# First image of an attention kernel: the next image's input load moves from unit 12 to unit 16, and its group-norm steps get new distances

## The chip, the cores and the metric

The kernel runs on one core of one Trainium2 chip. A core has a matrix engine (TensorE, "PE" in the profile, with its weight loads as "PEld"), three engines for elementwise work (VectorE "DVE", ScalarE "ACT", GpSimd "POOL"), and SyncE ("SP"), which issues DMA transfers. The metric is the device time of one execution in microseconds; lower is better. A unit below is a step of the kernel's inner loop, not a piece of hardware.

## The reference, cut to what matters

Eight images of 384 channels by 32x32 pixels pass through two attention layers; the second has a feed-forward part. The change touches the first layer alone:

```python
def _gn(v, G=32, eps=1e-5):
    g = v.reshape(B_, G, C_ // G, H_, W_)
    m = jnp.mean(g, axis=(2, 3, 4), keepdims=True)
    s = jnp.var(g, axis=(2, 3, 4), keepdims=True)
    return ((g - m) / jnp.sqrt(s + eps)).reshape(v.shape)
...
tokens = x.reshape(b, c, n).transpose(0, 2, 1)          # n = 1024 tokens, c = 384
qkv = (tokens @ qkv_w + qkv_b).reshape(b, n, 3, NUM_HEADS, HEAD_DIM)   # 8 heads of 48
attn = jnp.einsum('bhnd,bhmd->bhnm', q * scale, k)
attn = attn + _relative_bias(h, w, mlp_w1, mlp_b1, mlp_w2, mlp_b2)[None]
attn = jax.nn.softmax(attn, axis=-1)
out = jnp.einsum('bhnm,bhmd->bhnd', attn, v)
...
x = x + _L0_conv_ref(_gn(x), ...)
```

`_relative_bias` is a small network over the difference of two pixel positions. It gives one number for each head and each pair of row and column difference, so its whole output follows from a table of 8 x 63 x 63 values.

## The kernel before, in words

The program is one stream for each engine, written out by hand: the order in which the Python code calls operations is the order in which each engine gets them, and each engine works through its own stream in that order. Waits between engines are semaphores.

The first layer is `_layer0`. It handles the images one after the other. For each image it makes 32 units: 4 pairs of heads, times 2 halves of the 1024 queries, times 4 groups of 256 keys. In unit `i`, `scores` (L685 to L711) emits 16 matmuls on PE into two PSUM tiles `s` (L692), then the 16 matmuls of `weigh` for the unit two before (probabilities times v into `o`, L723), then for each of the two heads an add of the position bias on DVE (L703, `e<-s,grow`) and an exponential on ACT (L707). All PSUM tiles of this kind, 4 of them, come from one pool (`mm2`): two `s` tiles per unit and one `o` tile that lives for four units. So PE can only run one unit ahead of the adds on DVE. After the last key group of a query half, ACT copies one half of `o` out (L731) and DVE adds the other (L734).

Work beside the attention is hung into a list, `later`. `later.after(n, work)` calls `work` at the n-th `later.step()` from there, and each unit ends with one such step; what is registered during unit `i` with n = 1 is therefore called at the end of unit `i` itself. What is called at the end of a unit stands on every engine behind that unit's adds and exponentials. For the first image (b = 0) this is:

- The bias table turned into `grow`, the form the adds read. The 32 pieces (8 heads times 4) are loaded from DRAM with four DMAs each (`grow_load`, L486), and then reversed by one copy (`grow_turn`), on ACT for even pieces (L496) and on DVE for odd ones (L498). The last 16 pieces (0 to 15 below) are staged in slices of `oT`, the last four of them in two slices by turns, so that each must wait for the turn of the piece two before it. Piece 13 is loaded at the end of unit 12 and turned at the end of unit 14; piece 14 follows one unit later; piece 15 is loaded at the end of unit 14 and turned at the end of unit 16. Then there is nothing left of the table.
- The qkv weights are cut into three parts for later products (`_cut_weights`): the steps L108, L134, L112 and L142 on DVE, each in a unit of its own from unit 9 on, and stores to DRAM (L122).
- For each pair of heads, `divide` sends the softmax sums through DRAM (L749, L751, L756, L764), with a power (L752) and a multiplication (L768) on POOL.
- The next image: `load` (L343) issues three DMAs of 512 KB into `xn1`. `group_norm` (L501) returns seven steps: three that measure one third each with two statistics instructions on DVE (L513), the third of which also sends the statistics through DRAM to regroup them (L517, L521); `scatter`, which combines them (L527 on DVE, four small POOL instructions from L528) and sends scale and offset back through DRAM (L535, L539); and three that apply them to one third each on ACT (L551). At units 28, 29 and 31 `mask` (L108) reads the normalised image, and after the 32 units it is projected.

All DMAs named here are issued by SP, in one queue and in program order, each on one of eight completion semaphores in turn: a DMA waits until the one eight before it has landed.

Which units the seven steps fall in before: the load at unit 12 with distances 5, 6, 7, 10, 13, 14, 15 puts the measurements at the ends of units 16, 17 and 18, `scatter` at 21, the applications at 24, 25 and 26.

## Time and profile before

| | us |
|---|---|
| median of 3 runs | 2976.45 (2976.02 to 2978.29) |
| the profiled execution | 2973.66 |
| its span, first to last instruction | 2971.8 |
| PE busy in the span | 2940.6 (99%) |
| DVE busy | 1940.2 (65%) |
| ACT busy | 1507.2 (51%) |
| POOL busy | 489.8 (16%) |
| first image's 32 units | from about 75 to 193 in the span |

The median and the profiled execution are two different measurements: the span comes from the profiled one, which was 2.79 us below the median of the timed ones. Engine shares are averages over the whole program. Times with two decimals in the prediction are positions in the span, in us from its start. [...] the start of the first matmul of a unit is the useful mark.

### The profile page before, as it was taken

What the parts mean: (1) busy time and instruction counts of PE and PEld (TensorE: products, weight loads), DVE (VectorE), ACT (ScalarE), POOL (GpSimd) and SP (SyncE); (2) the same over time, 40 slices, a digit from 0 to 9 for tenths busy, and PEclk for the clock granted to TensorE, in tenths of its full rate; (3) what the DMA queues carried; (4) which work ended last, traced back from release to release, by engine and by line L of the source; (5) the groups of instructions that cost most, each with busy time, mean ns of one, the idle gap of its engine ahead of it and who ended that gap; (6) DMA issues with size and microseconds to landing.
All of it is one profiled execution on the core that took longest, in us unless ns stands there. A gap on an engine that the chain in (4) does not pass through costs nothing.

```text
span 2971.8 us, 47061 instructions
## 1 busy us (share of the span) xinstructions
PE 2940.6 (99%) x19370; PEld 1662.5 (56%) x19370; DVE 1940.2 (65%) x1937; ACT 1507.2 (51%) x1846; POOL 489.8 (16%) x312
## 2 busy tenths in 40 slices
PE   8999999999999999999999999999999999999998
PEld 3345555656565655644545656746747747655553
DVE  3775748575675747564565785775775775875756
ACT  2654626354453626354463564564564555564644
POOL 3020202111110202112202202301302302302020
PEclk9999999999999999999999999999999999999999
DMA  7532131312203130222411112202202112112111
GB/s 196 171 99 85 44 111 38 97 59 52 76 16 112 24 104 24 63 89 60 128 50 38 61 38 67 85 17 79 73 25 77 68 31 71 67 40 82 40 45 38
DMA packets 129520, 203.71 MB, mean 69 GB/s; under 512 B 61872, under 2 KB 79648, under 8 KB 128816
## 3 DMA queue, kind: packets, MB, share of 16 engines
q1 hardware_dynamic: 126032, 198.77, 22.9%
q8 instruction: 156, 2.56, 0.4%
q10 hardware_dynamic: 3264, 1.82, 0.2%
q14 instruction: 68, 0.56, 0.1%
HBM read 152.99 MB, written 38.51 MB: 64 GB/s over the span
## 4 chain that ended last, share of the span: by engine, by line
PE 91%; DVE 3%; DMA 2%; ACT 2%; issue 1%; SPq 0%; POOL 0%; DVEq 0%; ACTq 0%
PE s L692 15%; PE o L723 14%; PE s L1649 11%; PE o L1698 10%; PE pg L170 6%; PE y2p L1943 6%; PE y1p L1892 5%; PE pp L791 4%; PE pv L666 4%; PE pv L1586 4%; PE pm L170 3%; PE pp L1795 3%; PE pq L1438 1%; PE pq L572 1%; DMA rb<-rd 1%
## 5 line engine op out<-in xcount | busy, mean ns | idle before, releaser
L707 ACT ACTIVATE e<-e 128x1024 f32<-128x1024 f32 x512 | 535.3, 1057 | 357.0 <-DVE e L703 339.9
L703 DVE TENSOR_TENSOR e<-s,grow 128x1024 f32<-128x1024 f32 x512 | 601.2, 1218 | 164.4 <-PE s L692 156.5
L692 PE MATMUL s<-qk 48*64 48x512 f32 x4096 | 615.0, 592 | 7.6 <-DVE e L703 7.5
L723 PE MATMUL o<-e,v 64*64 64x512 f32 x4096 | 609.1, 590 | 0.0
L1660 ACT ACTIVATE e<-s,kc 128x512 f32<-128x512 f32 x768 | 463.9, 694 | 173.0 <-PE s L1649 163.4
L1649 PE MATMUL s<-qk,qk 64*64 64x512 f32 x3072 | 418.9, 592 | 1.8 <-DVE oT L1708 1.6
L1698 PE MATMUL o<-e,v 64*64 64x512 f32 x3072 | 414.5, 590 | 0.0
L692 PEld LDWEIGHTS s<-qk 48*64 48x64 f32 x4096 | 228.9, 132 | 250.9 <-issue 104.3
L723 PEld LDWEIGHTS o<-e,v 64*64 64x64 f32 x4096 | 244.8, 133 | 196.9 <-issue 113.8
L1649 PEld LDWEIGHTS s<-qk,qk 64*64 64x64 f32 x3072 | 154.0, 132 | 191.9 <-issue 109.2
L1675 DVE TENSOR_TENSOR t<-t,e 128x1024 f32<-128x1024 f32 x192 | 230.9, 1221 | 45.8 <-ACT e L1660 45.8
L1698 PEld LDWEIGHTS o<-e,v 64*64 64x64 f32 x3072 | 159.9, 133 | 168.9 <-issue 141.8
L752 POOL TENSOR_TENSOR inv<-sums,over 128x16 f32<-128x16 f32 x32 | 95.6, 2988 | 866.3 <-DMA sums<-sd 591.4
L1879 DVE TENSOR_REDUCE parts<-y 128x1 f32<-128x1024 f32 x75 | 89.7, 1217 | 103.4 <-ACT y L1876 103.0
L1672 DVE TENSOR_TENSOR t<-e,e 128x1024 f32<-128x1024 f32 x96 | 114.1, 1224 | 59.5 <-ACT e L1660 59.5
L1555 POOL TENSOR_TENSOR hc<-hc,rsqrt 128x32 f32<-128x32 f32 x24 | 138.2, 5757 | 2.0
L666 PE MATMUL pv<-wv,xn 128*128 128x384 f32 x384 | 128.9, 490 | 0.0
L1586 PE MATMUL pv<-wv,bx 128*128 128x384 f32 x384 | 128.3, 491 | 0.0
L1795 PE MATMUL pp<-oT,L_attn_proj_wT 128*128 128x512 f32 x288 | 126.3, 595 | 1.5 <-DVE oT L1761 1.5
L791 PE MATMUL pp<-oT,wp 128*128 128x512 f32 x288 | 125.7, 595 | 0.0
L650 DVE SCALAR_TENSOR_TENSOR qk<-pg,qk 128x1024 f32<-128x1024 f32 x42 | 51.5, 1225 | 112.8 <-PE pg L170 98.1
L1586 PEld LDWEIGHTS pv<-wv,bx 128*128 128x128 f32 x384 | 119.4, 314 | 9.8 <-ACT e L1660 4.1
(213 smaller groups left out, 3507.7 us busy)
## 6 DMA issues: line engine op xcount, KB each, us to landing
rb<-rd SPq DMA_DIRECT2D x110, 256.0 KB
wc<-there SPq DMA_DIRECT2D x25, 576.0 KB
wc<-cut SPq DMA_DIRECT2D x24, 576.0 KB
xn<-in_x_dram SPq DMA_DIRECT2D x24, 512.0 KB
res<-in_x_dram SPq DMA_DIRECT2D x24, 512.0 KB
x<-res SPq DMA_DIRECT2D x24, 512.0 KB
bx<-x SPq DMA_DIRECT2D x8, 1536.0 KB
rq<-hi SPq DMA_DIRECT2D x48, 256.0 KB
```

What stands on the lines that cost most here:

```text
L170: self.nc.tensor.matmul(out[:, h], w[:, i, k], part[k][:, ts(h, HALF)], start=(k == 0 and i != 1), stop=(k == KC - 1 and i != 0),)
L666: nc.tensor.matmul(pv[:, i, 0:C], xn[:, k, ts(2 * m2 + i, P)], wv[:, k, :], start=(k == 0), stop=(k == KC - 1),)
L692: nc.tensor.matmul(s[j][ts(c, QP), i], qk[pair][rows, 1, ts(4 * m2 + 2 * i + c, QP)], qk[pair][rows, 0, ts(h, HALF)], start=True, stop=True,)
L703: nc.vector.tensor_add(e.rearrange("p (i q) -> p i q", i=2), s[j], bass.AP(near.tensor, near.offset, [near.ap[0], [-QROWS * IW, 2], [1, HA ...
L707: nc.scalar.activation(e, e, AF.Exp)
L723: nc.tensor.matmul(po[ts(j, S0), r], v[keys, 2 * m2 + i, 2 * pair + j, :], es[j][keys, ts(i, HALF)], start=(m2 == 0 and i == 0), stop=(m2 ...
L791: nc.tensor.matmul(pps[b, m][:, h], (wp[:, k] if k < NF0 else wl)[:, ts(m, P)], oT[:, k, ts(h, HALF)], start=(k == 0), stop=(k == (NF0 if ...
L1586: nc.tensor.matmul(pv[:, i, 0:C], xt[:, k].rearrange("c (p m) -> c m p", m=MT)[:, 2 * m2 + i], wv[:, k], start=(k == 0), stop=(k == KC - 1),)
L1649: nc.tensor.matmul(s[j][ts(c, QP), i], qk[pair, 1][rows, ts(4 * m2 + 2 * i + c, QP)], qk[pair, 0][rows, ts(h, HALF)], start=True, stop=True,)
L1660: nc.scalar.activation(e[:, ts(i, HALF)], s[j][:, i], AF.Exp, scale=kc[:, pair, j, m : m + 1])
L1675: nc.vector.tensor_add(total[j], total[j], e)
L1698: nc.tensor.matmul(po[ts(j, D1), r], v[keys, 2 * m2 + i, at : at + D1], es[j][keys, ts(i, HALF)], start=(m2 == 0 and i == 0), stop=(m2 == ...
```

## The change

In the loop over the units of the first layer, for the first image alone, the load of the next image is issued at unit 16, not 12, and the seven steps of its group norm get shorter distances. Images from the second on keep their unit and their distances.

```diff
-                if i == (12 if b == 0 else 1) and b + 1 < B:
+                if i == (16 if b == 0 else 1) and b + 1 < B:
                     xn = load(b + 1)
                     for at, stage in zip(
-                        (5, 6, 7, 10, 13, *((14, 15) if b == 0 else (13, 13))),
+                        (3, 4, 5, 7, 9, 10, 11) if b == 0 else (5, 6, 7, 10, 13, 13, 13),
                         group_norm(b + 1, xn),
                     ):
                         later.after(at, stage)
```

The measurements come to the ends of units 18, 19 and 20 (16, 17 and 18 before), `scatter` to 22 (21 before), and the applications stay at the ends of 24, 25 and 26.

## The prediction

> **What bounds the kernel now.** The page first: PE carries the program.

> ```profile
> PE 2940.6 (99%) x19370; PEld 1662.5 (56%) x19370; DVE 1940.2 (65%) x1937; ACT 1507.2 (51%) x1846; POOL 489.8 (16%) x312
> PE 91%; DVE 3%; DMA 2%; ACT 2%; issue 1%; SPq 0%; POOL 0%; DVEq 0%; ACTq 0%
> L692 PE MATMUL s<-qk 48*64 48x512 f32 x4096 | 615.0, 592 | 7.6 <-DVE e L703 7.5
> ```

> So only PE's idle or slowed time can be won. Of its 7.5 us of waits before L692, the longest is 4.2. The waits between 105 and 200 us place it:

> ```profile
> DVE grow L498 <- DMA oT<-table: 4.9, 1, 4.9
> PE s L692 <- DVE e L703: 4.7, 2, 4.2
> SPq L486 <- DMA xn<-in_x_dram: 3.5, 3, 1.9
> ```

> DVE waited 4.9 us for one piece of the bias table, and PE then waited 4.2 us for DVE. The chain of waits has the same place on the path, and the timelines of DVE, PE and SP show what stood there:

> ```profile
> 125.28 6.37 DMA oT<-table
> ...
> 131.73 0.65 DVE L498 COPY grow<-oT 128x480 f32<-128x480 f32 x1 [4.92 <-DMA oT<-table]
> ...
> 128.38 0.59 PE L692 MATMUL s<-qk 48*64 48x512 f32 x1
> ...
> 133.57 2.83 PE L692 MATMUL s<-qk 48*64 48x512 f32 x11 [4.17 <-DVE e L703]
> ...
> 138.76 0.76 PE L692 MATMUL s<-qk 48*64 48x512 f32 x1
> ...
> 119.53 1.98 SPq L764 DMA_DIRECT2D rb<-rd  x2
> 121.94 1.31 SPq L343 DMA_DIRECT2D xn<-in_x_dram  x3
> 123.36 7.23 SPq L486 DMA_DIRECT2D oT<-table  x8
> ```

> Piece 13 (the first four of those eight L486 DMAs) was issued at 123.36 to 125.28, behind the three xn DMAs, and its last DMA landed 6.37 us later. Its turn at the end of unit 14 holds DVE, behind it wait the adds of unit 15, and behind them, for a PSUM tile, the scores of unit 16. The windows of one microsecond give the second half of the cost:

> ```profile
> 131.00:132.00 1.00, 0.00 (x0) 0.00 (x0) 0.27 (x1) 0.00 (x0) 0.00 (x0) 1.00 0.66 187
> 132.00:133.00 1.00, 0.00 (x0) 0.00 (x0) 1.00 (x2) 0.00 (x0) 0.00 (x0) 0.64 0.97 289
> 133.00:134.00 1.00, 0.43 (x4) 0.30 (x8) 1.00 (x2) 0.39 (x1) 0.00 (x0) 0.50 0.67 213
> 138.00:139.00 1.00, 1.00 (x12) 0.39 (x8) 1.00 (x2) 0.39 (x1) 0.00 (x0) 0.50 0.00 0
> 139.00:140.00 1.00, 1.00 (x12) 0.29 (x8) 1.00 (x2) 0.93 (x2) 0.00 (x0) 0.94 0.06 16
> ```

> (Columns: stretch, its length, busy time of PE, PEld, DVE, ACT and POOL, granted clock, DMA share, GB/s.) The clock fell to half at about 132.3 and came back at about 139.1, so PE worked at half speed for 5.5 us after it started again.

> [...] the DMAs of piece 14 wait on the semaphores of xn, and were issued at 126.67, 128.11 and 130.29, so the three thirds had landed 4.7, 5.7 and 7.4 us after their issues.

> **The change part by part.**

> *The load leaves unit 12.* The first scores matmul of a unit comes every 3.44 us where nothing disturbs (149.79, 153.23, 156.67). From unit 16's to unit 17's it took 138.76 - 128.38 = 10.38. The disturbance cost 6.94 us: the 4.17 of idle PE, plus half of 5.5 (2.75), which is 6.92. Would piece 13 be in time? Its DMAs now follow the rb DMAs at once (else they wait only for turn 11, done at 120.06): 121.6 to 123.3. rb had landed when POOL's multiplication started at 125.28. Bytes: 120 to 125 us moved 232 GB/s, 1.16 MB; what is due in front of and with piece 13 is two rb DMAs (0.52 MB), about 0.2 MB of piece 12 and its own 0.47 MB, so its last byte moves at about 125.1; before, data ended about 2 us ahead of the 131.65 landing; so it lands by about 127.2. The turn also carries a wait on POOL's multiplication into oT, which ended at 127.66. DVE reaches it at 126.8 (adds of unit 14: 124.46 + 2.36). The wait thus falls from 4.92 to 0.4 to 0.9; the turn (0.64) ends by about 128.3, against about 127.95 at which unit 15's adds are due. That is 0.3 late, nearly covered by the slack below. I charge 0.2, from 0 (landed by 126.8) to 1.5 (landed at 128.8). Pieces 14 and 15 have room: their issues wait for turns 12 (125.34) and 13 (128.3), last DMAs at about 127.1 and 130.1, plus 2 to 3 us, against turns at about 131.1 (ACT) and 133.9 (DVE).

> *The load enters unit 16.* On SP it now stands behind the weight store of unit 15 (L142 on DVE ends at about 130.7): issued at about 131.2 to 132.5, 1.3 us of issuing. With the landings seen (4.7, 5.7, 7.4), in company of piece 15, the thirds are there at 136, 137 and 139. DVE wants them after the adds of units 18, 19, 20: about 140.9, 144.4, 148. Nearly 5 us to spare, so 0; cover gone, each us beyond goes to DVE. Queued behind it on SP are the L749 DMAs of pair 1, which wait for DVE at the end of unit 17 anyway; the second rb DMA, a weight store and the statistics DMA now wait for the semaphores of xn, 10 us or more after its issue.

> *Measurements at 18, 19, 20 and scatter at 22.* The same six L513 (0.68 each, 1.2 a pair when chained) and one L527 (0.79, chained 0.71) move among other DVE work. Adds take 2.26 of a unit's 3.44, so 1.18 is free, and extra work pushes PE only past that and past about 0.45 of slack (scores end to first add's end 1.2, against 1.72 of weigh matmuls between). Excess over 1.18, before: unit 16 (turn 0.57 + pair 1.2) 0.59; 17 (L734 0.6 + 0.1 + pair) 0.72; 18, 0.02; sum 1.33, less slack 0.88. Unit 21 (0.1 + 0.6 + L134 0.87 + 0.71) 1.10, less slack 0.65. Together 1.5; measured, units 17 to 24 took 25.64 against 7 x 3.44 = 24.08, 1.56, of which about 0.28 belongs to the two o evictions, so 1.28. After: 18 and 19, 0.02 each; 20 (L108 0.46 + pair) 0.48; 21 (0.7 + 0.87) 0.39; 22 (L112 0.87 + 0.71) 0.40; sum 1.31, less one slack 0.86. Gain 0.4 to 0.7; I take 0.5, bounds 0 and 1.

> *Chains through DRAM.* The statistics' way from last L513 to the combined instruction took 4.9 us in image 0 (8.21 to 13.09, waiting); now the adds of two units, L734, L134 and L112 stand between, 6.9 us: 2.0 to spare. From L527 to the applied third it took 5.8 (13.09 to 18.88, waiting); now 24's exponentials end 10.3 after the adds of 22 start, and L527 starts at 3.1: 7.2, so 1.4 to spare. A late one would hold ACT only, two units ahead of the weigh matmuls. POOL's multiplication of pair 1 (2.4 to 3.7 us) now stands ahead of the four small ones; its rb lands about 2.7 us before it would matter. Cost 0 for all.

> *Sum.* -6.94 - 0.5 + 0.2 = -7.2. Span 2971.8 - 7.2 = 2964.6; its execution 2973.66 - 7.2 = 2966.5. The timed median lies 2.8 above that execution; I subtract from it as it is: 2976.45 - 7.2 = 2969.3.

> **Rivals.**

> *Half of it (gain 3 to 5.9).* [...] if the idle 4.17 us usually don't drop the clock in the timed runs, only 4.17 + 0.5 - 0.2 = 4.5 is there: 2972.0. Or piece 13 lands at 129 behind rb and its turn still holds DVE by over 1 us. [...] Against it: [...] the timed runs are no faster than the profiled one.

> *A new wait takes its place (slower).* If xn's first third needs more than 9.7 us from its issue, unit 18's measurement holds DVE as the turn did, and the clock may fall again. At 9.7 + 0.45 + 7.2 = 17 us it eats the gain; about 13 more on DVE than today's slack, 23 us in all, would make it slower by over 0.2%: 2983. Against it: 7.4 us for all three in a fuller queue, and 3.6 us for the first third at the start of the kernel (0.74 to 4.36).

> *It does nothing (2975 to 2977).* The chain would have to show the stall covered by something else that ends just then: POOL's multiplication ended at 127.66, four microseconds earlier. Little speaks for it.

> **How the numbers follow.** Full gain (6 to 8.5 us) 0.66; half 0.23; nothing 0.05; slower 0.06. A measurement tells about 0.2% from no change, 5.95 us here, so the full gain is just outside and half of it inside: faster 0.67, same 0.27, slower 0.06. The likeliest one's own range is 2968 to 2970.5. For 8 in 10 I take in the half case and a full gain with a longer slow-clock stretch in the timed runs (up to 6.8 us at half speed, 3.4): 2967 to 2974.

> **What would show it.** Right: no wait of L498 on the table over 1 us near 127, no PE wait of 4 us, granted clock 1.00 from 125 to 145, unit 16's to unit 17's scores 3.4 to 3.8 us, L513 without a DMA wait, units 18 to 24 with about 0.9 us over the pace. Wrong: DVE idle before L513, L527 or L498 by microseconds; a slow clock elsewhere; or everything as described and the timed median less than 5 us lower, which would say that the timed runs didn't pay the slow clock.

## The result, and the profile after

The changed kernel takes 2969.5 us in the median of nine runs (2967.66 to 2970.98). The kernel before, run beside it, takes 2976.45 in nine (2974.22 to 2979.95). The ratio is 0.9975, 95% interval 0.9964 to 0.9985, so the change makes the kernel 6.95 us faster; 2969.3 was predicted.

The two profiled executions show less than that: 2973.66 before and 2970.98 after, with spans of 2971.8 and 2969.1. The first lies below all nine runs of the kernel before, the second is the highest of the nine of the changed kernel. The first image is therefore compared stage by stage here; what may make executions scatter by microseconds comes at the end.

The page of the changed kernel, the lines that answer to those shown before:

```profile
PE 2939.3 (99%) x19370; PEld 1667.5 (56%) x19370; DVE 1941.8 (65%) x1937; ACT 1506.5 (51%) x1846; POOL 490.0 (17%) x312
PE 91%; DVE 3%; DMA 2%; issue 2%; ACT 1%; POOL 0%; SPq 0%; DVEq 0%; ACTq 0%; POOLq 0%
L692 PE MATMUL s<-qk 48*64 48x512 f32 x4096 | 612.2, 591 | 5.1 <-DVE e L703 5.0
```

PE still carries the program. The idle time in front of L692 fell from 7.6 to 5.1 and its busy time from 615.0 to 612.2: less waiting, and fewer matmuls at half clock (6.83 us of it in the first layer before, none now). It fell by less than the 4.2 of the stall because this execution has a wait of 1.5 us in a later image. The waits between 105 and 200 us (total, times, longest) show that the stall is gone:

```profile
DVE grow L498 <- DMA oT<-table: 0.9, 1, 0.9
PE s L692 <- DVE e L703: 0.4, 2, 0.2
```

DVE waits 0.9 us for piece 13, not 4.9; PE's longest wait for DVE is 0.2, not 4.2. The timelines of DVE, PE and SP (start, duration, engine, line) at the same place:

```profile
128.46 0.65 DVE L498 COPY grow<-oT 128x480 f32<-128x480 f32 x1 [0.92 <-DMA oT<-table]
...
141.43 1.28 DVE L513 BATCH_NORM_STATS2 gst<-xn 128x6 f32<-128x512 f32 x2
...
129.11 0.59 PE L692 MATMUL s<-qk 48*64 48x512 f32 x1
...
132.95 0.59 PE L692 MATMUL s<-qk 48*64 48x512 f32 x1
...
122.94 4.85 SPq L486 DMA_DIRECT2D oT<-table  x8
...
132.35 1.75 SPq L343 DMA_DIRECT2D xn<-in_x_dram  x3
```

From unit 16's first scores matmul to unit 17's it is 132.95 - 129.11 = 3.84 us (10.38 before). The image is issued at 132.35, and the measurement L513 at 141.43 starts without a wait. The windows of three microseconds (stretch, length, busy time of PE, PEld, DVE, ACT and POOL, granted clock, DMA share, GB/s):

```profile
128.00:131.00 3.00, 2.84 (x28) 0.82 (x24) 2.54 (x3) 1.36 (x2) 0.86 (x1) 1.00 0.91 247
131.00:134.00 3.00, 3.00 (x32) 1.08 (x28) 2.56 (x4) 2.34 (x4) 0.00 (x0) 1.00 0.77 230
134.00:137.00 3.00, 3.00 (x32) 0.92 (x24) 2.41 (x4) 1.71 (x2) 0.00 (x0) 1.00 1.02 325
```

The clock stays at 1.00 where it was 0.50 from about 132.3 to 139.1, and the DMA engines are no less busy than before (0.90 over these 9 us, 0.79 in the same ones before): the image now moves while nobody waits for it.

By stages of the first image, from first scores matmul to first scores matmul, with two later executions of the changed kernel that are told of below:

| us | before | after | after, again | after, third |
|---|---|---|---|---|
| unit 16 to 17 (the stall) | 10.38 | 3.84 | 3.44 | 3.44 |
| unit 17 to 25 (statistics) | 29.08 | 28.90 | 29.22 | 28.95 |
| gain of both | | 6.72 | 6.80 | 7.07 |

All of the gain is in the first row. The second one, from which the prediction wanted 0.5, gained 0.18, lost 0.14 and gained 0.13. Its ends are the first scores matmuls of units 17 and 25; that of unit 25 before, then after:

```profile
167.84 0.59 PE L692 MATMUL s<-qk 48*64 48x512 f32 x1
```

```profile
161.85 0.59 PE L692 MATMUL s<-qk 48*64 48x512 f32 x1
```

### The profile page after: what moved, and what is told of

It is laid out like the page before. It is cut to its first block, busy times and chain, and to the rows that moved or that the text cites. A ratio compares the mean times of both kernels' runs of the same rounds, so it can differ in the third digit from the quotient of the medians.

```text
span 2969.1 us, 47062 instructions
## 1 busy us (share of the span) xinstructions
PE 2939.3 (99%) x19370; PEld 1667.5 (56%) x19370; DVE 1941.8 (65%) x1937; ACT 1506.5 (51%) x1846; POOL 490.0 (17%) x312
## 4 chain that ended last, share of the span: by engine, by line
PE 91%; DVE 3%; DMA 2%; issue 2%; ACT 1%; POOL 0%; SPq 0%; DVEq 0%; ACTq 0%; POOLq 0%
PE s L692 14%; PE o L723 14%; PE s L1649 11%; PE o L1698 10%; PE pg L170 6%; PE y2p L1943 6%; PE y1p L1892 5%; PE pp L791 4%; PE pv L666 4%; PE pv L1586 4%; PE pm L170 3%; PE pp L1795 3%; PE pq L1438 1%; PE pq L572 1%; DMA rb<-rd 1%
## 5 line engine op out<-in xcount | busy, mean ns | idle before, releaser
L703 DVE TENSOR_TENSOR e<-s,grow 128x1024 f32<-128x1024 f32 x512 | 601.1, 1218 | 161.9 <-PE s L692 152.3
L692 PE MATMUL s<-qk 48*64 48x512 f32 x4096 | 612.2, 591 | 5.1 <-DVE e L703 5.0
L692 PEld LDWEIGHTS s<-qk 48*64 48x64 f32 x4096 | 229.0, 132 | 246.0 <-issue 101.0
L752 POOL TENSOR_TENSOR inv<-sums,over 128x16 f32<-128x16 f32 x32 | 96.0, 2999 | 857.5 <-DMA sums<-sd 584.8
L1586 PE MATMUL pv<-wv,bx 128*128 128x384 f32 x384 | 128.3, 491 | 0.0
```

The costliest lines, as they stand in the source:

```text
L692: nc.tensor.matmul(s[j][ts(c, QP), i], qk[pair][rows, 1, ts(4 * m2 + 2 * i + c, QP)], qk[pair][rows, 0, ts(h, HALF)], start=True, stop=True,)
L703: nc.vector.tensor_add(e.rearrange("p (i q) -> p i q", i=2), s[j], bass.AP(near.tensor, near.offset, [near.ap[0], [-QROWS * IW, 2], [1, HA ...
L1586: nc.tensor.matmul(pv[:, i, 0:C], xt[:, k].rearrange("c (p m) -> c m p", m=MT)[:, 2 * m2 + i], wv[:, k], start=(k == 0), stop=(k == KC - 1),)
```

## Experiments

The main theory: the three image DMAs, issued ahead of piece 13 of the bias table, delay that piece; its turn holds DVE, DVE holds PE, and the pause costs once more through the clock. The rivals: what helped is the new place of the statistics; or only the idle time is paid and not the clock; or the piece is late not because it stands behind the image in the queue but because both share the DMA engines' bandwidth. After a pause, half clock lasted 3.41 us (in the changed kernel, from 2034.84) or 6.83 (in the kernel before, from 132.28); a stretch of 3.41 is called a window of half clock below.

### One half of the edit at a time

The new units of the statistics (18, 19, 20 and 22), with the load left at unit 12:

```diff
-                        (5, 6, 7, 10, 13, *((14, 15) if b == 0 else (13, 13))),
+                        (7, 8, 9, 11, 13, 14, 15) if b == 0 else (5, 6, 7, 10, 13, 13, 13),
```

> The load stays at unit 12, only the group norm's steps take the new units (18, 19, 20, 22; applications as before). Main theory (the gain is the table piece freed from the image in front of it): the turn of piece 13 waits for the table 4.5 to 5.2 us as before, PE is idle about 4 us, the clock drops to half for one or two windows, and the time is that of the kernel before less 0 to 0.6 us: 2975.5 to 2977, no difference that can be measured. Rival (moving the statistics away from units 16 to 18 is what gains): 2969 to 2971.

Measured: 2976.97 us (13 runs), ratio to the kernel before 1.0002 (0.9994 to 1.001). The timelines of DVE and PE:

```profile
132.95 0.65 DVE L498 COPY grow<-oT 128x480 f32<-128x480 f32 x1 [5.33 <-DMA oT<-table]
...
134.79 2.83 PE L692 MATMUL s<-qk 48*64 48x512 f32 x11 [4.58 <-DVE e L703]
```

The stall is there in full, and the clock was at half for 6.83 us from 133.63. So the places of the statistics alone bring nothing that can be measured.

The load moved to unit 16, with the statistics left in their old units (16, 17, 18 and 21), so that the first measurement stands at the end of the unit that loads the image:

```diff
-                if i == (12 if b == 0 else 1) and b + 1 < B:
+                if i == (16 if b == 0 else 1) and b + 1 < B:
...
-                        (5, 6, 7, 10, 13, *((14, 15) if b == 0 else (13, 13))),
+                        (1, 2, 3, 6, 9, 10, 11) if b == 0 else (5, 6, 7, 10, 13, 13, 13),
```

> The load goes to unit 16, the steps keep their old units (16, 17, 18, 21). Main theory: the turn of piece 13 waits about 0.9 us as in the changed kernel, but the first measurement now stands behind a third of the image that was issued about 3 us before: DVE waits 1.5 to 3 us for it at unit 16 and little at 17, PE idles 1 to 2.5 us, perhaps with one window of half clock (up to 1.7 us more): 2 to 4 us above the changed kernel, 2971 to 2974. Rival (the load's place is all, the distances don't matter): within 1 us of the changed kernel, 2969 to 2970.5.

Measured: 2972.79 us (21 runs), ratio 0.9988 (0.9981 to 0.9994). Piece 13's turn doesn't wait at all. That turn on DVE, then DVE and PE a little later (the profiled execution, 2976.85 us, is the slowest of the 21):

```profile
126.93 0.64 DVE L498 COPY grow<-oT 128x480 f32<-128x480 f32 x1
...
136.05 1.29 DVE L513 BATCH_NORM_STATS2 gst<-xn 128x6 f32<-128x512 f32 x2 [1.78 <-DMA xn<-in_x_dram]
...
138.51 2.05 PE L692 MATMUL s<-qk 48*64 48x512 f32 x11 [2.03 <-DVE e L703]
```

and the windows of three microseconds there:

```profile
136.00:139.00 3.00, 0.97 (x14) 0.22 (x10) 2.95 (x4) 1.10 (x2) 0.00 (x0) 1.00 0.52 201
139.00:142.00 3.00, 3.00 (x20) 1.61 (x16) 2.94 (x5) 1.61 (x2) 0.00 (x0) 0.56 0.01 3
```

The old wait is gone and the rival "a new wait takes its place" shows itself in small: the measurement at the end of unit 16 comes 1.8 us before its third has landed, PE stands for 2.03 and then runs at half clock for one window of 3.41. That is 2.03 + 3.41 / 2 = 3.7 us by the profile; the medians of this kernel and of the changed one differ by 3.3. So the new distances are worth nothing alone and about half of the gain together with the new load: they give the transfer its time. The image was issued at 131.25, so its first third took at most 4.8 us; in the changed kernel (issue at 132.35, first L513 at the end of unit 18) that leaves over 4 us.

### Which transfer is in whose way

Image 1's DMAs issued by ACT in place of SP, at the old unit 12:

```diff
+            queue = nc.scalar if b == 1 else nc.sync
...
-                nc.sync.dma_start(t[:, k], x[b, ts(k, P)].rearrange("p h w -> p (h w)"))
+                queue.dma_start(t[:, k], x[b, ts(k, P)].rearrange("p h w -> p (h w)"))
```

> The kernel before with one edit: the three DMAs of the second image's load are issued by ACT instead of SP, still at unit 12. Ring order (piece 13 is late because it stands behind the image in SP's own queue): the turn's wait falls to 1 us or less and the time to 2969.5 to 2971. Shared bandwidth (piece 13 is late because 1.5 MB more are moved in the same microseconds): both queues take turns on the DMA engines, piece 13 lands 1.5 to 3.5 us later than in the changed kernel, the turn waits 2.5 to 4 us, and the time is 2972 to 2976.

Measured: 2975.42 us (12 runs), ratio 0.9998 (0.9989 to 1.0006). The timelines of ACT's and SP's issues, and DVE's (one line was added, so numbers are one higher):

```profile
119.48 2.66 ACTq L344 DMA_DIRECT2D xn<-in_x_dram  x3
...
117.59 6.53 SPq L487 DMA_DIRECT2D oT<-table  x4
...
132.61 0.65 DVE L499 COPY grow<-oT 128x480 f32<-128x480 f32 x1 [5.92 <-DMA oT<-table]
```

The wait is longer, not gone. But the run doesn't separate a queue's order from a shared bandwidth, as it was meant to: SP now needed 6.53 us for the four DMAs of piece 12 (1.70 otherwise), because the last of them waited 5.0 us for an image DMA. The eight completion semaphores are common to both queues, so a DMA of SP still waits for the one before it on its semaphore, whichever queue that is in. SP's waits between 110 and 140 us (total, times, longest):

```profile
SPq L487 <- DMA xn<-in_x_dram: 6.1, 2, 5.0
```

The second of these two waits held one of piece 13's own DMAs, until 128.1. Piece 13 was issued from 125.95 on, in place of 123.36. Inconclusive by its times; what its packets show comes below.

The load right behind piece 13 in SP's queue, at the end of unit 12, with the statistics in their old units:

```diff
-                if i == (12 if b == 0 else 1) and b + 1 < B:
+                if b > 0 and i == 1 and b + 1 < B:
...
                 later.step()
...
+                if b == 0 and i == 12:
+                    xn = load(1)
+                    for at, stage in zip((4, 5, 6, 9, 12, 13, 14), group_norm(1, xn)):
+                        later.after(at, stage)
```

> The load is issued at the end of unit 12, behind piece 13 of the table but ahead of pieces 14 and 15; steps at their old units (16, 17, 18, 21). Ring order: turn 13 on DVE waits 0.5 to 1.2 us; piece 14 is late instead, its turn on ACT waits 1 to 3 us, which costs PE nothing (exponentials are needed two units later); piece 15 waits on DVE 0 to 2 us. Time 2969.5 to 2972. Shared bandwidth: turn 13 still waits 2 us or more, and the time is above 2972.

Measured: 2975.24 us (12 runs), ratio 0.9996 (0.9987 to 1.0004): a miss. SP, DVE and PE:

```profile
123.11 1.61 SPq L343 DMA_DIRECT2D xn<-in_x_dram  x3
...
128.39 4.96 SPq L486 DMA_DIRECT2D oT<-table  x4
...
127.43 0.65 DVE L498 COPY grow<-oT 128x480 f32<-128x480 f32 x1 [0.66 <-DMA oT<-table]
...
136.69 0.65 DVE L498 COPY grow<-oT 128x480 f32<-128x480 f32 x1 [3.08 <-DMA oT<-table]
...
139.71 2.83 PE L692 MATMUL s<-qk 48*64 48x512 f32 x11 [3.34 <-DVE e L703]
```

Piece 13 is in time (0.66 us of waiting) although the image is issued only 2 us after it: what delays a piece is the image ahead of it. But ACT then waited 2.2 us for piece 14, and piece 15, whose four DMAs took 4.96 us to issue behind the semaphores of the image, is late by 3.08. PE stood for 3.34 us and ran at half clock for 6.83. The stall moved on by one piece of DVE's. The image has to be behind the whole table, whose last four DMAs go out at the end of unit 14 (129.14 in the changed kernel).

Only a part of the image ahead of piece 13: one third of it, or two, at unit 12, and the rest at 16 (statistics as in the changed kernel; the diff is to that kernel, with `range(2)` for two thirds):

```diff
-        def load(b):
-            t = shared.image(f"xn{b}")
-            for k in range(KC):
+        def load(b, some=range(KC), t=None):
+            t = shared.image(f"xn{b}") if t is None else t
+            for k in some:
...
+                if b == 0 and i == 12:
+                    early = load(1, range(1))
...
-                    xn = load(b + 1)
+                    xn = load(1, range(1, KC), early) if b == 0 else load(b + 1)
```

> The changed kernel with one third of the image (one DMA of 512 KB) issued at unit 12 and two at unit 16. Main theory (piece 13 waits for the bytes in front of it in its queue, in proportion): the turn waits 1.5 to 2.8 us, between the 0 to 0.9 with nothing in front and the 4.9 to 5.3 with three thirds; PE idles 0.7 to 2 us, perhaps with one window of half clock; 2970.5 to 2973.5. Rival (a step: any DMA of the image in front brings nearly the whole wait): the turn waits 4 us or more, 2975 or above.

> The same with two thirds at unit 12 and one at unit 16. Main theory: the turn waits 3 to 4.2 us, PE idles 2.3 to 3.5 us, the clock drops for one or two windows; 2973 to 2976. Rival (a step): as before, the turn waits 4.5 us or more, 2975.5 or above.

Measured: 2973.62 us for one third (12 runs; ratio 0.999, 0.9982 to 0.9999) and 2975.38 for two (12 runs; 0.9991, 0.9982 to 0.9999). The turn of piece 13 on DVE, with one third and then with two:

```profile
129.72 0.65 DVE L498 COPY grow<-oT 128x480 f32<-128x480 f32 x1 [2.24 <-DMA oT<-table]
```

```profile
131.72 0.65 DVE L498 COPY grow<-oT 128x480 f32<-128x480 f32 x1 [4.92 <-DMA oT<-table]
```

More of the image in front means a longer wait: 0 to 0.92 us without any (seven executions), 2.24 with 0.5 MB, 4.92 with 1 MB. With all 1.5 MB it is 4.92 and 5.33, no longer than with two thirds, so it isn't proportional: by its wait one third met the expectation (its median lies 0.1 us above the range), and two thirds met the rival's 4.5 us or more. The windows of two thirds:

```profile
125.00:128.00 3.00, 3.00 (x32) 0.90 (x28) 1.80 (x2) 2.44 (x3) 2.38 (x1) 1.00 0.96 286
128.00:131.00 3.00, 1.39 (x16) 0.23 (x8) 0.00 (x0) 0.00 (x0) 0.00 (x0) 1.00 0.62 143
```

286 GB/s became 143. Why the rate fell, and so why the last DMA of piece 13 took that long there, isn't settled by these runs. With one third PE stood for 1.49 us and kept its clock in the profiled execution, 2971.79 us, one of the kernel's faster ones.

The DMA packets of the traces say where the piece's bytes stood. A packet of the table has 3656 bytes, one of the image or of `rb` (the inverted softmax sums, ahead of the image on SP) 4096. In the kernel before, where piece 13 was issued from 123.36 on, no table packet began between 122.11 and 127.50, while 412 of the others did; with the new steps alone there was none between 122.52 and 128.98, and 478 of the others. With two thirds of the image in front it was 229 between 122.27 and 125.70, with one third 180 between 123.06 and 126.07. With the image in ACT's queue, 28 table packets began from 125.0 to 126.5 while 95 of the image did. So in one queue the piece's bytes stood behind the image's and did not take turns with them, and from two queues they did mix.

### Where the statistics' half microsecond went

A first attempt spread the six measuring instructions more evenly: load at the end of unit 14 behind piece 15, one L513 at 17, two at 18, two at 19, one at 20, the combining step at 23, applications at 25 to 27.

```diff
+                if b == 0 and i == 14:
+                    xn = load(1)
+                    for at, stage in zip(
+                        (3, 4, 4, 5, 5, 6, 9, 11, 12, 13), group_norm(1, xn, True)
+                    ):
+                        later.after(at, stage)
```

> Meant to beat both: the load at the end of unit 14, right behind the last table piece, and the six statistics instructions put one to unit 17, two to 18, two to 19, one to 20, the combination to 23, the applications to 25, 26, 27. By the DVE account (1.18 us free in each unit beside the adds) no unit but 21 (1.57) is over, and the slack of about 0.45 holds that: the scores of units 17 to 25 keep the pace of 3.44 us but for the o evictions and about 0.2 us, where the changed kernel lost 1.19 us at units 22 to 24. 0.7 to 1.2 us below the changed kernel run beside it, 2968 to 2969. Rival (those losses were not DVE's): within 0.3 us of the changed kernel.

> The changed kernel once more, as the neighbour of the other three and for a second profile: 2968.5 to 2970.5; the turn of piece 13 waits 0 to 1 us, unit 16's to unit 17's scores 3.4 to 3.9 us, no slow clock between 120 and 200 us. A slow clock or a wait of over 1.5 us there would show the first profile to be an exception.

Measured beside each other: 2969.73 us spread (10 runs; ratio 0.9974, 0.9964 to 0.9983) and 2969.26 for the changed kernel again (9 runs; 0.9975, 0.9965 to 0.9985): no difference in time, where 0.7 to 1.2 less was expected. Units 17 to 25 took 28.67 us spread, where 29.22 was measured for the changed kernel again: 0.55 better, with 0.97 still lost in one place, from unit 23 to 24. The timelines of POOL and DVE there, first of the changed kernel, then of its second execution, then of the spread one (ten lines were added ahead, so its L778 is L768):

```profile
151.03 2.39 POOL L768 TENSOR_TENSOR oT<-oT,rb 128x1024 f32<-128x1024 f32 x1 [6.16 <-DMA rb<-rd]
...
152.84 1.40 DVE L134 TENSOR_TENSOR w<-w 128x768 f32<-128x768 f32 x1
```

```profile
150.94 2.39 POOL L768 TENSOR_TENSOR oT<-oT,rb 128x1024 f32<-128x1024 f32 x1 [6.36 <-DMA rb<-rd]
...
152.43 1.71 DVE L134 TENSOR_TENSOR w<-w 128x768 f32<-128x768 f32 x1
```

```profile
150.86 2.38 POOL L778 TENSOR_TENSOR oT<-oT,rb 128x1024 f32<-128x1024 f32 x1 [6.20 <-DMA rb<-rd]
...
152.15 1.91 DVE L134 TENSOR_TENSOR w<-w 128x768 f32<-128x768 f32 x1
```

L134 took 0.95 us in the kernel before. Here it takes 1.40, 1.71 and 1.91: longer, the earlier it starts. What stays the same is the distance of the two ends: 154.24 - 153.42 = 0.82, 154.14 - 153.33 = 0.81, 154.06 - 153.24 = 0.82. So nearly all of the 0.95 us that L134 took before comes after the end of POOL's multiplication, whenever L134 begins: beside L768 it stands still. What holds it, these traces don't show. In the kernel before, the two were apart, but there L768 met L112. POOL and DVE before:

```profile
162.28 3.67 POOL L768 TENSOR_TENSOR oT<-oT,rb 128x1024 f32<-128x1024 f32 x1
176.99 3.58 POOL L752 TENSOR_TENSOR inv<-sums,over 128x16 f32<-128x16 f32 x1 [11.04 <-DMA sums<-sd]
...
158.97 0.95 DVE L134 TENSOR_TENSOR w<-w 128x768 f32<-128x768 f32 x1
...
162.76 0.94 DVE L112 SCALAR_TENSOR_TENSOR cd<-w 128x768 f32<-128x768 f32 x1
...
176.71 0.95 DVE L112 SCALAR_TENSOR_TENSOR cd<-w 128x768 f32<-128x768 f32 x1
```

Here POOL is the one that stands: L768 took 3.67 in place of 2.38, although its record begins 0.48 us before L112's, so the order of the recorded starts doesn't tell which of the two will stand. So did the power L752, which takes 2.90 alone: begun while L112 ran, it ended 2.91 us after L112 in all twelve executions where the two met, whenever it had begun.

Two kernels test it by moving L134 and the two steps behind it one unit later, to 22, 23 and 24; the first is the changed kernel with this alone, the second the spread one with it:

```diff
-            for at, stage in zip(((9, 11, 13, 15), (20, 21, 22, 23), (24, 25, 26, 27))[k], stages):
+            for at, stage in zip(((9, 11, 13, 15), (20, 22, 23, 24), (24, 25, 26, 27))[k], stages):
```

> The changed kernel, with the subtraction L134 of the second weight part at the end of unit 22 in place of 21, and the two steps behind it, L112 and L142, one unit later each. In the changed kernel L134 took 1.40 and 1.71 us in two executions in place of 0.95, and each time it ended 0.81 to 0.82 after POOL's multiplication L768. [...] L134 stands still while L768 runs, and that ate the gain of the statistics' new places. Then here L134 starts about 2 us after L768 has ended and takes 0.95, and the scores go from unit 17's first matmul to unit 25's in 28.1 to 28.4 us, against 28.90 and 29.22 in the changed kernel and 29.08 in the one before; the time is 0.5 to 1.0 us below the changed kernel's, which its scatter of 1 us in the median nearly hides. Rival, the DVE account alone: the loss is in the work of units 20 to 22 itself, as counted, and moves with it; L134 takes 1.4 or more in its new place too, or 17 to 25 stays at 28.8 to 29.2.

> The kernel with the six statistics instructions spread over units 17 to 20, with the same shift of L134, L112 and L142 by one unit. There L134 took 1.91, ending 0.82 after L768, and units 17 to 25 took 28.67. [...] L134 takes 0.95, 17 to 25 takes 27.6 to 27.9, and the time is 1.0 to 1.6 us below the changed kernel's. Rival, the DVE account alone: 28.4 to 28.7 and no time below that of the kernel with the spread alone.

> The changed kernel once more, beside these two on the same chip: 2969 to 2970, L134 between 1.3 and 2.0 us, ending 0.8 after L768, units 17 to 25 in 28.8 to 29.3.

POOL and DVE with the shift alone, then with both:

```profile
149.74 2.38 POOL L768 TENSOR_TENSOR oT<-oT,rb 128x1024 f32<-128x1024 f32 x1 [6.82 <-DMA rb<-rd]
...
153.42 0.95 DVE L134 TENSOR_TENSOR w<-w 128x768 f32<-128x768 f32 x1
```

```profile
150.01 2.38 POOL L778 TENSOR_TENSOR oT<-oT,rb 128x1024 f32<-128x1024 f32 x1 [6.17 <-DMA rb<-rd]
...
154.09 0.95 DVE L134 TENSOR_TENSOR w<-w 128x768 f32<-128x768 f32 x1
```

| one chip | median us (runs) | ratio to before (95%) | L134 | units 17 to 25 |
|---|---|---|---|---|
| changed kernel, third | 2968.89 (9) | 0.9978 (0.9968 to 0.9988) | 1.45 | 28.95 |
| L134 later | 2968.68 (10) | 0.9975 (0.9966 to 0.9985) | 0.95 | 28.14 |
| spread and L134 later | 2967.40 (7) | 0.9969 (0.9958 to 0.9981) | 0.95 | 27.70 |

Clear of L768, L134 is back at 0.95, and both stages fall where they were expected if L134 stands still beside L768. The duration of L134 is what tells: the first variant's stage fell by 0.81 from that of the changed kernel's third execution, more than the 0.50 by which L134 had been longer there, so some of it comes from the new spacing of the steps. Eight units without any disturbance would be 8 x 3.44 = 27.52. In the third execution of the changed kernel the two ends are again 0.82 apart (L768 ended at 151.57, L134 at 152.39). In the whole time this is small: the first variant's 0.2 us, where 0.5 to 1.0 was expected, is no difference. The second variant has the lowest median of all kernels run, 1.5 below the changed kernel's and 8.3 below the kernel before's of 2975.66 on that chip, but its interval overlaps the changed kernel's: that it beats the kernel before is shown, that it beats the changed kernel is shown by the stage alone.

## Why the prediction was right, and where it was not

- *The load leaves unit 12 (-6.94).* Right. The stage gave 6.54, 6.94 and 6.94 in three executions, and the load left at unit 12 kept all of the stall. The split into idle time and clock is right too: in all five profiled kernels that had a pause of 3.3 us or more there, the clock was at half for 6.83 us afterwards.
- *Turn 13 (+0.2, waiting 0.4 to 0.9).* It waited 0.92, 0 and 0.19 us in the three executions and cost 0.4, 0 and 0: in size right. One reason given for it was wrong: the turn does not wait for POOL's multiplication into `oT`. In the changed kernel it started at 128.46, while L768 ran from 126.48 to 128.86.
- *The load enters unit 16 (0).* Right: issued at 132.35 (131.2 to 132.5 predicted), no L513 waits. The spare time is real but not generous: two units earlier the wait is 1.8 us and costs 3.7.
- *Statistics (-0.5).* This term failed: -0.18, +0.14 and -0.13 were measured. The account of DVE's free time was sound, but it took L134 at 0.87 in the new place. It noted that POOL's multiplication of pair 1 moves and asked only who waits for its result, not what it does to its neighbour on DVE. Measured gain plus the excess of L134 over 0.95 is 0.18 + 0.45, -0.14 + 0.76 and 0.13 + 0.50, that is 0.63, 0.62 and 0.63: the gain was there, near its predicted size, and the standstill of L134 took it back.
- *Chains through DRAM (0).* Right: no wait of L527 or L551 stands in the changed kernel's trace between 105 and 200 us.
- *Sum.* -7.2 predicted; the stages give -6.72, -6.80 and -7.07, the medians -6.95, -7.48 (2969.26 against 2976.74) and -6.77 (2968.89 against 2975.66).
- *Rivals.* "Half of it" rested on a clock that usually stays up in the timed runs, which was the author's assumption; the medians gained 6.8 to 7.5 where it allowed 4.5, so they contain the clock's share, and it is out for this stall. "A new wait" didn't occur, but the load alone shows how near it was. "Nothing" is what the statistics alone gave.

- *Luck.* The median came within 0.2 us of the prediction, closer than the working deserves: the half microsecond that the statistics did not give is as large as the difference between the medians of the changed kernel in its three sets of runs, 2969.50, 2969.26 and 2968.89.

That a piece is late through the image ahead of it is shown (4.92 and 5.33 us with it ahead, 0 to 0.92 without), and the packets show that its bytes wait behind the image's in the queue. The traces don't tell the DMA engines apart, so in what order each single engine took them isn't shown.

## What to carry to other kernels

A big prefetch belongs behind the last small transfer that holds up a chain like that of piece 13 (4.92 us on DVE, then 4.17 on PE), and its first user has to move along by as much; either half of such an edit alone may bring nothing or create the next stall. Price a pause of the matrix engine with the clock behind it, which here was 2.75 us on top of 4.17. When steps are re-timed, check which POOL instruction each DVE step will meet, not only which data it needs: L134 took up to 1.91 us beside L768 in place of 0.95. Where POOL was the one that stood, DVE lost nothing: L112 took 0.94 and 0.95.

## What was not expected of the hardware

*Short pauses can drop the clock too.* Pauses of 2.03, 1.87, 1.73 and 1.56 us each were followed by exactly one window of 3.41 us at half clock in these traces, while pauses of 1.84, 1.75, 1.71, 1.65, 1.54 and 1.49, among others, were not; the five pauses of 3.34 to 5.16 us each brought two. The changed kernel's own profile has one, in the second layer, far from the change. The timeline of PE and the windows there:

```profile
2034.15 2.31 PE L170 MATMUL pm<-xd,wc 128*128 128x512 f32 x6 [1.87 <-DMA wc<-there]
```

```profile
2032.00:2034.00 2.00, 0.28 (x2) 0.00 (x0) 1.32 (x2) 1.45 (x3) 0.00 (x0) 1.00 0.34 139
2034.00:2036.00 2.00, 1.85 (x6) 1.51 (x7) 2.00 (x2) 0.99 (x1) 0.00 (x0) 0.71 0.00 0
2036.00:2038.00 2.00, 2.00 (x7) 1.54 (x6) 2.00 (x3) 1.50 (x2) 0.00 (x0) 0.50 0.00 0
```

Two or three such places per execution would make a scatter of some microseconds, which is what all kernels here show (2972.0 to 2980.2 in 49 runs of the kernel before). The mean granted clock of the timed runs fits: in 104 runs of the kernel before on three chips, the 14 with 0.997 took 2978.8 us on average, the 85 with 0.998 took 2976.4, and the 5 with 0.999 took 2974.5; a thousandth of the clock over 2972 us is 3.0. That short pauses are the cause was not tested.

*Of a DVE step and a POOL step that meet, one stands still.* In seven executions of five kernels L134 started while L768 ran, and ended 0.81 to 0.82 us after it, whenever it had started. Not every such meeting costs: in the changed kernel a later L112, begun at 199.84, took its usual 1.22 beside L752, which ran from 199.47 and took 2.89. Why neither of these two stood still is open.

*Completion semaphores tie queues together.* In these kernels a transfer moved to another queue still held SP for 5.0 us, through a semaphore that both use.
